# Fetching more table rows by address, and categories by one-hot products, in a deep-interest recommender kernel

## The chip, the cores and the metric

The kernel runs on one core of a Trainium2 chip. The metric is device time in microseconds (us) of one execution, the median of several. A core has five engines that run their own instruction streams: TensorE (PE, matrix products; PEld is its weight load), VectorE (DVE), ScalarE (ACT), GpSimd (POOL) and SyncE (SP). SP, ACT and POOL also issue DMAs.

## The reference

There are B = 16,384 users, each with a history of L = 200 items, one candidate item and one category; all are ids into tables of embeddings of D = 64 floats.

```python
def dice(x, alpha, axis):                 # normalised over the users
    mean = jnp.mean(x, axis=axis, keepdims=True)
    var = jnp.var(x, axis=axis, keepdims=True)
    p = jax.nn.sigmoid((x - mean) * jax.lax.rsqrt(var + EPS))
    return x * (p + alpha * (1.0 - p))
u, it, c, h = u_emb[user], i_emb[item], c_emb[cate], i_emb[hist]
itb = jnp.broadcast_to(it[None], h.shape)
feat = jnp.concatenate([h, itb, h - itb, h * itb], axis=-1)
a = dice(feat @ au_W1 + au_b1, au_alpha, axis=1)
w = a @ au_W2 + au_b2
cur = jnp.sum(w * jax.lax.stop_gradient(h), axis=0)
z = jnp.concatenate([u, it, c, cur], axis=-1)
z = dice(z @ W1 + b1, alpha1, axis=0)
z = dice(z @ W2 + b2, alpha2, axis=0)
return z @ W3 + b3
```

What matters here: 200 x 16,384 rows of 256 bytes come from the item table at random places (ids up to 100,000), and 16,384 each from the item, category and user tables once. The statistics of each l need all users of that l.

## The kernel before, in words

The users are 128 tiles of 128 rows. A step k takes 16 of them (TD = 16) for one l; 8 steps (ND = 8) make an l, and K = 1600 steps the loop. LAG = 10 further steps drain it.

Step k issues (`step`, L421): the id list of the next l (`load_hist_ids`), `fetch(k)` (L344), the load of the candidate rows of step k + 1 (`load_items`, L391, 512 KB from HBM by SP), `turn(k-1)` (L381: DVE transposes the rows into hT, ACT copies them to PSUM), `hidden` and `measure` of step k - 3 (L373, L376), once in 8 steps `moments` (L399: mean and variance, then `scale_and_shift` L166 with Sqrt on ACT), `gate(k-10)` (L350: two activations on ACT), `product(k-1)` (L394: PE, with DVE's product hm between its halves), and `weights` and `weigh` of step k - 10 (L355, L368, all on DVE). The schedule is manual: each engine runs its instructions in the order in which the code gives them.

A step's rows come in two ways. `gather` (L125) is an indirect DMA that POOL issues, 128 rows of 256 bytes by a column of ids. For three of the 128 tiles of each l (`SIDES`), rows come one by one by address: the ids are loaded on one partition (`load`, L293), DVE multiplies them by the row's size (`scale`, L296), the engine loads addresses into registers (L301) and issues one DMA of 256 bytes per row (L312 on SP, L323 on ACT). SP does two tiles of each l (`BY_SP`) and ACT one (`BY_ACT`); ACT then copies the finished tile into the step's buffer (L387). SP's rows use the eight rotating semaphores that its DMAs have; ACT's rows count into semaphores of their own (`landed`). ACT issues its rows in a step between `gate` and `product`. So 15 gathers are left in a step that has a side tile, and 16 in the others.

Before the loop (L474) 128 gathers fetch the candidates' rows into two buffers in turn, which are transposed, stored to HBM as `items`, and multiplied by their part of the first layer (`itp`). After it, the head fetches 16 groups of 16 gathers, categories and users in turn (`head_fetch`, L505), into three buffers, while the last steps drain. `head_layer` (L520) multiplies: for a category group the products of category, candidate and `cur`, for a user group those of the user and then the activations and statistics. The rest of the head (from L552) is a chain of normalisations, two dice layers, and the output DMAs.

Of the kernel before, what the change touches and what calls it, by code (L numbers as in the profile page):

```python
# [26 lines left out]
SIDES = (1, 5, 6)  # L27
PERIOD = 1
BY_SP = ((0, 1), (0, 5))
BY_ACT = ((0, 6),)  # L30
# [5 lines left out]
def din_kernel(  # L36
# [34 lines left out]
    NS = len(SIDES)  # L71
    NC = NT - NS
# [17 lines left out]
    def column(c, n):  # L90
        if c in SIDES and n == TD - 1:
            return NC + SIDES.index(c)
        return c * TD + n - sum(s < c for s in SIDES)

    def columns(v):
        return v[: NC * P].rearrange("(p n) -> p n", n=NC)

# [8 lines left out]
    items = [dram.tile([P, CD], F32, name=f"items{c}") for c in range(ND)]  # L106
    cur = [make(f"cur{c}", P, CD) for c in range(ND)]
# [5 lines left out]
    ucT = itp[:4]  # L113
    idx = [make(f"idx{i}", P, NT, dt=I32) for i in range(IDX)]
    ids = [make(f"ids{i}", P, NT, dt=I32) for i in range(3)]
    side = [make(f"side{i}", P, D) for i in range(3)]
    aside = [make(f"aside{i}", P, D) for i in range(2)]
    addr = [make(f"addr{i}", 1, P, dt=I32) for i in range(3)]
    aaddr = [make(f"aaddr{i}", 1, P, dt=I32) for i in range(2)]
    landed = [tc.alloc_semaphore(f"landed{i}") for i in range(2)]  # L120
# [12 lines left out]
    def load_ids(t, v):  # L133
        nc.sync.dma_start(t[:, :NC], columns(v))
        for s in range(NS):
            nc.sync.dma_start(t[:, NC + s : NC + s + 1], col(v[(NC + s) * P : (NC + s + 1) * P]))

    def load_hist_ids(i, l, by_address):
        nc.sync.dma_start(
            idx[i][:, :NC], r_hist[ds(l, 1), : NC * P].rearrange("l (p n) -> p (l n)", n=NC)  # L140
        )
        for s, c in enumerate(SIDES):
            if c not in by_address:
                j = NC + s
                nc.sync.dma_start(
                    idx[i][:, j : j + 1], r_hist[ds(l, 1), j * P : (j + 1) * P].rearrange("l p -> p l")
                )
# [18 lines left out]
    def scale_and_shift(mean, var, rstd, shift):  # L166
        n = mean.shape[0]
        std = small.tile([P, 1], F32, tag="std", name="std")
        nc.scalar.activation(std[:n], var, AF.Sqrt, bias=eps[:n])
        nc.vector.reciprocal(rstd, std[:n])  # L170
        nc.vector.scalar_tensor_tensor(shift, mean, -1.0, rstd, ALU.mult, ALU.mult)

    eps = make("eps", P, 1)
# [11 lines left out]
    def attention_weights():  # L185
        nc.vector.memset(eps, EPS)
# [36 lines left out]
    same_b = make("same_b", P, P)  # L223
    lanes, lane = (rows[-2].rearrange("p n d -> p (n d)")[:, (5 + i) * P : (6 + i) * P].bitcast(I32) for i in range(2))

    def head_weights():
# [21 lines left out]
        nc.sync.dma_start(bias3, b3.partition_broadcast(P))  # L248
        for t, u in ((ala, al1a), (alb, al1b), (al2, al12)):
            nc.vector.tensor_scalar(u, t, -1.0, 1.0, ALU.mult, ALU.add)  # L250
# [8 lines left out]
    class Queue:  # L259


        def __init__(self, engine, tiles, group, lead, span, buffers, addresses):
            self.engine, self.tiles, self.group, self.lead, self.span = engine, tiles, group, lead, span
            self.buffers, self.addresses, self.n = buffers, addresses, len(buffers)
            self.per = P // group
            self.plan = None

        def line(self, m):
            p, t = divmod(m, len(self.tiles))
            return p * PERIOD + self.tiles[t][0]  # L270

# [4 lines left out]
        def when(self, q):  # L276
            m, i = divmod(q, self.per)
            return m * PERIOD * ND // len(self.tiles) + i * self.span // self.per - self.lead

        def events(self, k, count):  # L280
            if self.plan is None:
                self.plan = {}
                for m in range(count):
                    at = self.when(m * self.per)
                    self.plan.setdefault(at - 8, []).append((self.load, m))
                    self.plan.setdefault(at - 5, []).append((self.scale, m))
                for q in range(count * self.per):
                    self.plan.setdefault(self.when(q), []).append((self.fetch, q))
            return self.plan.get(k, ())

        def load(self, m):
            j = NC + SIDES.index(self.tiles[m % len(self.tiles)][1])
            nc.sync.dma_start(self.addresses[m % self.n], r_hist[ds(self.line(m), 1), j * P : (j + 1) * P])  # L293

        def scale(self, m):
            nc.vector.tensor_scalar_mul(self.addresses[m % self.n], self.addresses[m % self.n], ROW)  # L296

        def fetch(self, q):
            m, part = divmod(q, self.per)
            p0 = part * self.group  # L300
            _, at = nc.values_load_multi_w_load_instructions(  # L301
                self.addresses[m % self.n][:, p0 : p0 + self.group],
                engines=(self.engine,), min_val=0, max_val=ROW * (V - 1),
                skip_runtime_bounds_check_because="the DMA checks the address against the table",
            )
            for j, a in enumerate(at):
                row = flat[ds(a, ROW)].rearrange("(o d) -> o d", o=1)
                self.start(m, self.buffers[m % self.n].bitcast(U8)[p0 + j : p0 + j + 1], row)

    class SyncQueue(Queue):  # L310
        def start(self, m, dst, row):
            nc.sync.dma_start(dst, row)  # L312

        def take(self, m):
            return self.buffers[m % self.n]

    class ScalarQueue(Queue):
# [3 lines left out]
        def start(self, m, dst, row):  # L321
            key = self.opened.setdefault(m, f"rows{next(self.names)}")
            dma = nc.scalar.dma_start(dst, row).then_inc(landed[m % self.n], 16)  # L323
            tc.no_tile_sem_insts.add(dma.ins.name)
            tc.add_to_no_dep_group(key, dma.ins)

        def take(self, m):
            fence = nc.scalar.wait_ge(landed[m % self.n], 16 * P)
            tc.declare_fence(fence.ins, group=self.opened.pop(m))
            nc.scalar.sem_clear(landed[m % self.n])  # L330
            return self.buffers[m % self.n]

    by_sync = SyncQueue(mybir.EngineType.SP, BY_SP, 16, 8, 4, side, addr)
    by_scalar = ScalarQueue(mybir.EngineType.Activation, BY_ACT, 8, 4, 8, aside, aaddr)
    queues = (by_sync, by_scalar)

    def by_address(l):
        return {c for q in queues for t, c in q.tiles if t == l % PERIOD}

    def has_side(k):  # L340
        l, c = divmod(k, ND)
        return c in by_address(l)

    def fetch(k):  # L344
        l, c = divmod(k, ND)
        for n in range(TD - has_side(k)):
            j = column(c, n)
            gather(rows[k % ROWS], idx[l % IDX][:, j : j + 1], n, i_emb)

    def gate(k):  # L350
        i = k // ND % 3
        nc.scalar.activation(pg, xs[k % XR], AF.Sigmoid, bias=shifts[i], scale=rstds[i])  # L352
        nc.scalar.activation(pg, pg, AF.Identity, bias=au_al, scale=au_1al)  # L353
# [27 lines left out]
    def turn(k):  # L381
        if has_side(k):
            l, c = divmod(k, ND)
            for q in queues:
                m = q.tile(l, c)
                if m is not None:
                    nc.scalar.copy(rows[k % ROWS][:, TD - 1], q.take(m))  # L387
# [11 lines left out]
    def moments(l):  # L399
# [17 lines left out]
        scale_and_shift(mean, var, rstds[i], shifts[i])  # L417
# [3 lines left out]
    def step(k):  # L421
# [4 lines left out]
        rows_by_scalar = ask(k)  # L426
        if has(k):
            l, c = divmod(k, ND)
            if c == 0 and l + 1 < L:
                load_hist_ids((l + 1) % IDX, l + 1, by_address(l + 1))  # L430
            fetch(k)
        if has(k + 1):
            load_items(k + 1)
        if has(k - 1):
            turn(k - 1)
        if has(k - 3):
            hidden(k - 3)
            measure(k - 3)
            if (k - 3) % ND == ND - 1:
                moments((k - 3) // ND)  # L440
        if has(k - LAG):
            gate(k - LAG)
        for q in rows_by_scalar:
            by_scalar.fetch(q)
# [6 lines left out]
    def ask(k):  # L451
        late = []
        for q in queues:
            for what, m in q.events(k, L * len(q.tiles) // PERIOD):
                if q is by_scalar and what == q.fetch:
                    late.append(m)
                else:
                    what(m)
        return late

    with tc.manual_schedule():
        load_ids(ids[0], r_item)
        load_hist_ids(0, 0, by_address(0))
        load_ids(ids[1], r_cate)
        load_ids(ids[2], r_user)
        nc.gpsimd.iota(lanes, pattern=[[1, P]], base=P, channel_multiplier=-1)
# [207 lines left out]
```

## Time and profile before

| | |
|---|---|
| Time, median of 3 runs | 31,799.49 us (31,797.17 to 31,803.53) |
| The profiled execution, its own time | 31,801.04 us |
| Its span, first to last instruction | 31,799.3 us |
| Busy: POOL, DVE, PE, ACT | 23,955.0, 22,816.1, 9,881.5, 6,126.3 us |
| POOL's gathers in the loop | 25,000 |
| POOL's gathers of candidates, categories, users | 128 each |
| Row DMAs by SP and by ACT | 51,200 and 25,600 |
| Item loads of 512 KB by SP | 1,608 |
| Granted TensorE clock, mean | 0.630 |

The profile shows one execution. A group's line gives the line of the code, the engine, the operation, what it writes and reads, how many, the busy time and mean of one, and the idle time of the engine just before them with what ended it ("issue": nothing that the profile shows was waited for). In the timeline a line has start, duration, engine, line and operation; neighbours of one kind are put together with their count, and SPq and ACTq are the issuing of DMAs. The waits view gives total us, times and the longest.

### The profile page before, as it was taken

How to read it: one execution, taken by the hardware profiler on the slowest of the kernel's cores; microseconds unless marked ns; L12 is line 12 of the kernel's file. 1: busy time of each engine (PE TensorE's matmuls, PEld its weight loads, DVE VectorE, ACT ScalarE, POOL GpSimd, SP SyncE). 2: the span in 40 equal slices, each digit the busy share in tenths (PEclk: the TensorE clock that was granted, in tenths of full speed). 3: DMA queues.
4: the chain of work that ended last, by engine and by line, in shares of the span. 5: the costliest groups of instructions: out<-in, count | busy, mean ns of one | idle time of the engine just before them, and what ended most of it. 6: DMA issues, size and time to landing. Idle time of an engine off the chain costs nothing.

```text
span 31799.3 us, 270304 instructions
## 1 busy us (share of the span) xinstructions
PE 9881.5 (31%) x13196; PEld 3707.9 (12%) x13196; DVE 22816.1 (72%) x32088; ACT 6126.3 (19%) x6061; POOL 23955.0 (75%) x25389
## 2 busy tenths in 40 slices
PE   2333333333333333333333333333333333333334
PEld 0111111111111111111111111111111111111111
DVE  5777777777777777777777777777777777777776
ACT  1111111111111111111111111111111111111111
POOL 7777777777777777777777777777777777777776
PEclk6666666666666666666666666666666666666666
DMA  2222222222222222222222222222222222222221
GB/s 56 55 54 55 55 54 55 55 55 55 54 55 55 55 54 55 55 55 54 55 55 55 54 55 55 54 55 55 55 54 55 55 55 54 55 55 55 54 55 41
DMA packets 1237919, 1731.75 MB, mean 54 GB/s; under 512 B 622320, under 2 KB 622920, under 8 KB 1235912
## 3 DMA queue, kind: packets, MB, share of 16 engines
q0 software_dynamic: 812288, 833.41, 15.1%
q1 hardware_dynamic: 371704, 874.34, 8.1%
q14 instruction: 1904, 15.60, 0.2%
q10 hardware_dynamic: 51920, 6.72, 0.1%
q8 instruction: 103, 1.69, 0.0%
HBM read 1708.09 MB, written 4.33 MB: 54 GB/s over the span
## 4 chain that ended last, share of the span: by engine, by line
POOL 59%; issue 22%; DMA 9%; DVE 7%; ACT 2%; SPq 1%; PE 0%; ACTq 0%; DVEq 0%; POOLq 0%
POOL rows L126 59%; DMA rows<-in_L_rec_i_emb,idx 9%; DVE hT L155 2%; DVE xs L374 1%; DVE st L379 1%; DVE pg L357 1%; ACT L352 1%; DVE py L358 1%; DVE py L356 1%; DVE py L370 1%; ACT pg L352 1%; ACT pg L353 1%; DVE pg L362 0%; DVE other L406 0%; SPq L312 0%
## 5 line engine op out<-in xcount | busy, mean ns | idle before, releaser
L126 POOL DMA_INDIRECT rows<-in_L_rec_i_emb,idx x25000 | 23592.1, 944 | 7625.2 <-issue 7297.1
L160 PE MATMUL px<-hT,blk_h 128*128 128x512 f32 x6400 | 5959.6, 1086 | 21047.3 <-DVE xs L374 21026.7
L155 DVE STREAM_TRANSPOSE hT<-rows 64x512 f32<-64x512 f32 x6400 | 4515.5, 706 | 7173.2 <-DMA rows<-in_L_rec_i_emb,idx 6913.2
L389 ACT COPY py<-hT 128x1024 f32<-128x1024 f32 x1600 | 1626.3, 1016 | 20747.7 <-DVE hT L155 20695.1
L160 PEld LDWEIGHTS px<-hT,blk_h 128*128 128x128 f32 x6400 | 1876.3, 323 | 24165.5 <-DVE xs L374 22491.3
L160 PE MATMUL px<-hm,blk_m 128*128 128x512 f32 x6400 | 3969.7, 753 | 519.7 <-DVE hm L396 519.7
L356 DVE TENSOR_TENSOR py<-pg,xs 128x1024 f32<-128x1024 f32 x1600 | 1972.6, 1233 | 594.6 <-ACT pg L353 446.9
L160 PEld LDWEIGHTS px<-hm,blk_m 128*128 128x128 f32 x6400 | 1757.4, 278 | 3422.8 <-issue 1871.7
L379 DVE BATCH_NORM_STATS2 st<-xs 128x6 f32<-128x512 f32 x3200 | 2058.5, 685 | 55.0
L357 DVE STREAM_TRANSPOSE pg<-py 128x1024 f32<-128x1024 f32 x1600 | 2024.5, 1265 | 55.5
L396 DVE TENSOR_TENSOR hm<-py,itT 128x1024 f32<-128x1024 f32 x1600 | 1932.7, 1208 | 147.8 <-DMA itT<-items 111.1
L358 DVE TENSOR_REDUCE py<-pg 128x32 f32<-128x1024 f32 x1600 | 1972.7, 1233 | 54.4
L370 DVE TENSOR_TENSOR py<-rows,pg 128x1024 f32<-128x1024 f32 x1600 | 1966.1, 1229 | 54.8
L371 DVE TENSOR_TENSOR cur<-py,cur 128x1024 f32<-128x1024 f32 x1600 | 1958.5, 1224 | 55.2
L374 DVE TENSOR_TENSOR xs<-px,itp 128x1024 f32<-128x1024 f32 x1600 | 1959.6, 1225 | 50.5
L352 ACT ACTIVATE pg<-xs,sh,rs 128x1024 f32<-128x1024 f32 x1600 | 1925.6, 1203 | 60.7 <-DVE py L370 58.1
L353 ACT ACTIVATE pg<-pg,au_al,au_1al 128x1024 f32<-128x1024 f32 x1600 | 1883.4, 1177 | 53.7
L362 DVE SCALAR_TENSOR_TENSOR pg<-py,au_bias,part 32x16 f32<-32x16 f32 x6400 | 1529.4, 239 | 225.6
L387 ACT COPY rows<-side 128x64 f32<-128x64 f32 x400 | 97.7, 244 | 2573.1 <-DMA side<-in_L_rec_i_emb 2559.8
L359 DVE COPY part<-py 64x32 f32<-64x32 f32 x1600 | 310.6, 194 | 55.5
L387 ACT COPY rows<-aside 128x64 f32<-128x64 f32 x200 | 48.8, 244 | 1265.4 <-DMA aside<-in_L_rec_i_emb 1265.4
L352 ACT ACT_TABLE_LOAD x200 | 256.6, 1283 | 3.5
(129 smaller groups left out, 1892.8 us busy)
## 6 DMA issues: line engine op xcount, KB each, us to landing
itT<-items SPq DMA_DIRECT2D x1608, 512.0 KB
side<-in_L_rec_i_emb SPq DMA_DIRECT2D x51200, 0.2 KB
aside<-in_L_rec_i_emb ACTq DMA_DIRECT2D x25600, 0.2 KB
rows<-in_L_rec_i_emb,idx POOLq DMA_INDIRECT x25000
idx<-in_r_hist SPq DMA_DIRECT2D x200, 62.5 KB
addr<-in_r_hist SPq DMA_DIRECT2D x400, 0.5 KB
items<-itT SPq DMA_DIRECT2D x8, 512.0 KB
aaddr<-in_r_hist SPq DMA_DIRECT2D x200, 0.5 KB
```

Source lines behind the costliest of these rows:

```text
L126: nc.gpsimd.indirect_dma_start(out=dst[:, n, :], out_offset=None, in_=table, in_offset=bass.IndirectOffsetOnAxis(ap=ids, axis=0),)
L155: nc.vector.transpose(by_tile(dst[ts(e, D)], i)[:, n0:n1], of[ts(i, D), n0:n1, ts(e, S)])
L160: nc.tensor.matmul(dst[:, ts(i, CH)], lhsT, rhs[:, ts(i, CH)], start=(first and j == 0), stop=(last and j == len(pairs) - 1), skip_group_c ...
L352: nc.scalar.activation(pg, xs[k % XR], AF.Sigmoid, bias=shifts[i], scale=rstds[i])
L353: nc.scalar.activation(pg, pg, AF.Identity, bias=au_al, scale=au_1al)
L356: nc.vector.tensor_mul(py, pg, xs[k % XR])
L357: nc.vector.transpose(pg, py)
L358: nc.vector.reduce_sum(total, pg.rearrange("p (n a) -> p n a", a=S), axis=mybir.AxisListType.X)
L370: nc.vector.tensor_mul(of, rows[k % ROWS], w.unsqueeze(2).to_broadcast([P, TD, D]))
L371: nc.vector.tensor_add(cur[k % ND], py, cur[k % ND])
L374: nc.vector.tensor_add(xs[k % XR], px[k % 2], itp[k % ND])
L379: nc.vector.bn_stats(stats[l % 3][:, 2 * c + i, :], xs[k % XR][:, ts(i, CH)])
```

## The change

**Rows by address.** The pattern repeats over four l (`PERIOD`): SP takes 11 tiles in it and ACT 11, so 5.5 tiles of each l. A step has at most one side tile. Addresses come in groups of 32 registers, rows are issued 7 steps ahead (`AHEAD`) at an even rate of 44 rows a step on each queue (`until`, `pump`), into 5 buffers per queue (`SLOTS`), with 4 id lists (`LISTS`). Id lists are now strided loads, since the tiles keep one common layout (which also takes the special columns out of `load_ids` and out of the output DMAs). On ACT, `gate` moves ahead of the turn, with 5 rows between its activations and 5 behind; the remaining rows follow the turn's copy. The copy of a finished tile is `place(k)`, in step k itself. In the step with `moments` the gate comes after them and after 20 rows.

**The root.** `root` computes 1/sqrt by an integer start and four Newton rounds, 15 small operations on DVE, in place of ACT's Sqrt and DVE's reciprocal.

**The categories.** They are no longer gathered in the head. In the prologue, between the candidates' groups, 16 halves (`category`) are each 2 products that spread the category numbers over the partitions, 16 comparisons on DVE that make ones and zeros, and 16 products of those with the table. The results are stored in HBM (`cates`) and loaded again in the head as `cT`. The candidates' rows take eight buffers rather than two.

**The head.** Eight groups of user gathers over four buffers; the products of what is known (`head_known`) and of the users (`head_users`) follow one another for each group; w1b's products come ahead of w1a's, and the first dice layer of group c + 1 is issued ahead of the products of group c.

```diff
-SIDES = (1, 5, 6)
-PERIOD = 1
-BY_SP = ((0, 1), (0, 5))
-BY_ACT = ((0, 6),)
+PERIOD = 4
+BY_SP = tuple((t, c) for t in range(PERIOD) for c in (0, 3, 6) if (t, c) != (3, 0))
+BY_ACT = tuple((t, c) for t in range(PERIOD) for c in (1, 4, 7) if (t, c) != (1, 1))
+GROUP = 32
+AHEAD = 7
+SLOTS = 5
+LISTS = 4
...
+    def root(dst, var):
+        n, w = var.shape
...
+        nc.vector.tensor_single_scalar(v, var, EPS, ALU.add)
+        nc.vector.tensor_single_scalar(t.bitcast(I32), v.bitcast(I32), 1, ALU.logical_shift_right)
+        nc.vector.tensor_scalar(dst.bitcast(I32), t.bitcast(I32), -1.0, float(0x5F3759DF), ALU.mult, ALU.add)
+        for _ in range(4):
+            nc.vector.tensor_mul(t, dst, dst)
+            nc.vector.scalar_tensor_tensor(t, t, -0.5, v, ALU.mult, ALU.mult)
+            nc.vector.scalar_tensor_tensor(dst, t, 1.5, dst, ALU.add, ALU.mult)
...
+        def until(self, k):
+            return min(self.total * P, max(0, int((k + AHEAD) * self.rate)))
+        def pump(self, upto):
+            while self.done < upto:
+                m, r = divmod(self.done, P)
+                if r % GROUP == 0:
+                    _, self.at = nc.values_load_multi_w_load_instructions(
+                        self.lists[m % LISTS][:, r : r + GROUP],
...
+                row = flat[ds(self.at[r % GROUP], ROW)].rearrange("(o d) -> o d", o=1)
+                self.start(m, self.slots[m % SLOTS].bitcast(U8)[r : r + 1], row)
+                self.done += 1
...
+    def place(k):
+        if side(k):
+            q, m = side(k)
+            nc.scalar.copy(rows[k % ROWS][:, TD - 1], q.take(m))
+    def gate(k, between):
...
+        between()
...
+        by_sync.pump(by_sync.until(k + 1))
+        norm = has(k - 3) and (k - 3) % ND == ND - 1
+        if has(k - LAG) and not norm:
+            gate(k - LAG, lambda: some(5))
+            some(5)
+        if has(k):
+            place(k)
         if has(k - 1):
             turn(k - 1)
         if has(k - 3):
             hidden(k - 3)
             measure(k - 3)
...
+        if norm:
+            moments((k - 3) // ND)
+            some(20)
+            if has(k - LAG):
+                gate(k - LAG, lambda: some(5))
+        by_scalar.pump(by_scalar.until(k + 1))
...
+    def category(c, i):
+        to = py[:, ts(i, CH)]
+        r = i * ND + c
+        for g in range(2):
+            said = pg[:, ts(g, CH)]
+            nc.tensor.matmul(
+                said.rearrange("p (n t) -> p n t", t=S), chosen[r // ND][:, r % ND],
+                numbers.rearrange("r (g t n) -> r g n t", g=2, n=TD)[:, g],
+                start=True, stop=True,
+            )
+            for k in range(NK):
+                ones = equal[next(turns_of_equal) % len(equal)]
+                nc.vector.tensor_scalar(ones, said, of_row[:, k : k + 1], None, ALU.is_equal)
+                nc.tensor.matmul(
+                    to, spread[k // 4][:, k % 4, g], ones,
+                    start=(g == 0 and k == 0), stop=(g == 1 and k == NK - 1),
+                )
+        nc.scalar.copy(xs[c % XR][:, ts(i, CH)], to)
...
-                    gather(rows[c % 2], ids[0][:, j : j + 1], n, i_emb)
+                    gather(rows[c], ids[0][:, j : j + 1], n, i_emb)
...
+            if c < ND:
+                category(*halves_of.pop(0))
+            before(c - ND - 1)
...
+        for c in range(ND):
+            nc.sync.dma_start(cates[c], xs[c % XR])
...
+        k, c = K, 0
+        for j in range(ND):
+            head_fetch(j)
+            nc.sync.dma_start(cT[j % 4], cates[j])
+            load_items(K + j)
+            while k <= K + (j + 1) * LAG // ND:
+                step(k)
+                k += 1
+            while c <= j and k > K + LAG - ND + c:
+                head_known(c)
+                head_users(c)
+                c += 1
```

More of the change, by code (lines that the diff above doesn't have):

```diff
@@ L112, in din_kernel @@
     itp = [make(f"itp{c}", P, CD) for c in range(ND)]
-    ucT = itp[:4]
+    uT, cT = itp[4:8], itp[:4]
     idx = [make(f"idx{i}", P, NT, dt=I32) for i in range(IDX)]
[L115 to L120, printed above, removed]
+    ids = [make(f"ids{i}", P, NT, dt=I32) for i in range(2)]
+    landed = [tc.alloc_semaphore(f"landed{i}") for i in range(SLOTS)]
     stats = [make(f"st{i}", P, 2 * ND, STATS) for i in range(3)]
@@ L424, in has, with some @@
             return 0 <= j < K
-        rows_by_scalar = ask(k)
+        def some(n):
+            by_scalar.pump(min(by_scalar.done + n, by_scalar.until(k + 1)))
+        for q in queues:
+            q.lead(k)
         if has(k):
@@ L449, in step @@
             weigh(k - LAG)
[L451 to L459, printed above, removed]
+    NK = -(-c_emb.shape[0] // P)
+    flat_tile = lambda t: t.rearrange("p n d -> p (n d)")
+    numbers = flat_tile(rows[8])[: 2 * ND]
+    chosen = [flat_tile(rows[9 + i])[: 2 * ND].rearrange("r (j m) -> r j m", m=P) for i in range(2)]
@@ L467, in din_kernel @@
         attention_weights()
[L468 to L469 removed]
+        category_numbers()
         for t in cur:
@@ L472, in din_kernel @@
         head_weights()
+        ahead = [-16]
+        halves_of = [(c, i) for c in range(ND) for i in range(2)]
         for c in range(ND + 1):
```

298 lines of the change are left out of this document (129 added, 169 removed).

## The prediction

> **What bounds the kernel now.** I read the page first: engine totals, the chain that ended last, the costliest group.
>
> ```profile
> span 31799.3 us, 270304 instructions
> PE 9881.5 (31%) x13196; PEld 3707.9 (12%) x13196; DVE 22816.1 (72%) x32088; ACT 6126.3 (19%) x6061; POOL 23955.0 (75%) x25389
> POOL 59%; issue 22%; DMA 9%; DVE 7%; ACT 2%; SPq 1%; PE 0%; ACTq 0%; DVEq 0%; POOLq 0%
> L126 POOL DMA_INDIRECT rows<-in_L_rec_i_emb,idx x25000 | 23592.1, 944 | 7625.2 <-issue 7297.1
> ```
>
> POOL is busy 75%, but the idle time ahead of its gathers is nearly all "issue": it waits for nobody. A gather therefore costs (23592.1 + 7625.2)/25000 = 1.2487 us, and 25,000 of them make 31,217.3 of the 31,799.3 us. Next the groups with shapes kept apart, for the gathers outside the loop:
>
> ```profile
> L126 POOL DMA_INDIRECT rows<-in_L_rec_i_emb,ids x128 | 120.9, 945 | 49.6 <-issue 36.9 <-DVE itT L155 9.3 <-DMA ids<-in_r_item 1.9
> L126 POOL DMA_INDIRECT rows<-in_L_rec_u_emb,ids x128 | 120.8, 944 | 39.0 <-issue 36.9 <-DMA rows<-in_L_rec_u_emb,ids 2.1
> L126 POOL DMA_INDIRECT rows<-in_L_rec_c_emb,ids x128 | 120.8, 944 | 39.0 <-issue 37.2 <-DMA rows<-in_L_rec_c_emb,ids 1.8
> ```
>
> These are 170.5, 159.8 and 159.8 us. With the loop: 31,707.4. One step of the loop in the timeline, then the waits, say what stands beside POOL:
>
> ```profile
> 10007.19 2.87 DVE L155 STREAM_TRANSPOSE hT<-rows 64x512 f32<-64x512 f32 x4 [5.56 <-DMA rows<-in_L_rec_i_emb,idx]
> ...
> 10012.28 1.18 ACT L353 ACTIVATE pg<-pg,au_al,au_1al 128x1024 f32<-128x1024 f32 x1
> ...
> 10013.14 6.32 ACTq L323 DMA_DIRECT2D aside<-in_L_rec_i_emb  x16
> ...
> 10014.95 2.85 PE L160 MATMUL px<-hm,blk_m 128*128 128x512 f32 x4
> ...
> 10020.29 1.22 DVE L371 TENSOR_TENSOR cur<-py,cur 128x1024 f32<-128x1024 f32 x1
> ...
> 10027.33 2.86 DVE L155 STREAM_TRANSPOSE hT<-rows 64x512 f32<-64x512 f32 x4 [5.82 <-DMA rows<-in_L_rec_i_emb,idx]
> ```
> ```profile
> SPq L392 <- DVE hm L396: 7403.9, 1381, 21.5
> DVE hT L155 <- DMA rows<-in_L_rec_i_emb,idx: 6913.2, 1459, 12.2
> SPq L312 <- DMA side<-in_L_rec_i_emb: 254.9, 781, 0.8
> ```
>
> DVE works from 10007.19 to 10021.51, 14.3 us, and then sits 5.82 us until the next gathers have landed: it has room. SP waits 7403.9 us, 4.63 us a step, for DVE before an item load: room too, and the question is whether the change uses it up.
>
> **The loop.** Before, 3 tiles of each l come row by row; now 5.5. That removes 2.5 x 200 = 500 gathers, 500 x 1.2487 = 624.3 us, if POOL stays the bound: 15.3125 gathers, 19.12 us a step, instead of 19.51. What pays is SP and ACT: 44 rows a step each, where they had 32 and 16. Their paces:
>
> ```profile
> 10013.69 2.11 ACTq L323 DMA_DIRECT2D aside<-in_L_rec_i_emb  x7
> 10015.49 5.34 SPq L312 DMA_DIRECT2D side<-in_L_rec_i_emb  x16
> 10133.21 12.35 SPq L312 DMA_DIRECT2D side<-in_L_rec_i_emb  x32
> ```
> ```profile
> L301 SPq TENSOR_LOAD <-addr x3200: 1132/1226/1472, 181.0 to 31191.3; - x189
> L301 ACTq TENSOR_LOAD <-aaddr x3200: 711/787/1017, 195.1 to 31301.8; - x189
> ```
> ```profile
> L392 SPq DMA_DIRECT2D itT<-items x1608: 319/360/394, 176.7 to 31585.2; - x179
> ```
> ```profile
> L136 SPq DMA_DIRECT2D ids<-in_r_item x3: 420/424/432, 1.2 to 2.2; - x3
> ```
>
> - SP: a row is 5.34/16 = 0.334 us while ACT issues as well. Addresses come in groups of 32 now: SP's 16 took 1.226 us and ACT's 8 took 0.787, so a register is about 0.055 us and a group of 32 about 2.1 us (estimate). 44 x 0.334 + 1.375 x (2.1 + 0.17 of gap, estimate) + 0.36 for the item load and as much as 0.17 around it + 0.344 lists at the 0.43 of L136's strided loads and the ids = 14.7 + 3.1 + 0.5 + 0.2 = 18.5 to 18.6 us. The bound is 19.12, so SP fits with 0.5 us to spare. The third row, 12.35 us for 32 with one register load of about 1.3 inside, gives 0.345 a row and 19.1 to 19.2 us: that end costs nothing to 130 us over the loop. I take 18.6, the pace of the commoner row. The 4.63 us wait for DVE that covered SP's work is then gone.
> - ACT: 2.11/7 = 0.30, with the gaps 0.3135 a row; 44 rows 13.8 us, registers 1.375 x 2.4 = 3.3, small things 0.4: 17.5. Its three large operations (3.4 us) are on top only if they do not run beside the issuing. The row above shows that they do: rows start at 10013.14, while L353 runs until 10013.46. The other end, all 3.4 us on top, is 20.9 us and would make ACT the bound; I take the first, since the row shows the overlap, and 5 rows are now put between and behind the activations.
> - DVE: `root` puts 15 small operations (about 3.0 us) where ACT's Sqrt was, and one list scaling per tile, about 0.5 us a step together, inside the 5.82 us of idle time. ACT loses two table loads per l, off the path: nothing.
> - Buffers: rows are asked for 7 steps ahead, with 5 buffers per queue; `place` takes them at step k. A late row would hold ACT, behind it the copy L389, and behind that the products and DVE; that is rival C.
>
> **The head.** The windows show 319 us of head gathers, then the end:
>
> ```profile
> 31389.00:31708.00 319.00, 148.85 (x256) 45.27 (x256) 163.47 (x238) 42.96 (x38) 241.08 (x256) 0.70 0.17 36
> 31708.00:31800.00 92.00, 56.28 (x116) 22.40 (x116) 55.45 (x81) 37.95 (x38) 0.54 (x1) 0.82 0.02 2
> ```
> ```profile
> 31403.57 1.22 DVE L371 TENSOR_TENSOR cur<-py,cur 128x1024 f32<-128x1024 f32 x1
> ...
> 31413.57 1.22 DVE L371 TENSOR_TENSOR cur<-py,cur 128x1024 f32<-128x1024 f32 x1
> ...
> 31426.71 1.23 DVE L356 TENSOR_TENSOR py<-pg,xs 128x1024 f32<-128x1024 f32 x1 [3.37 <-ACT pg L353]
> ...
> 31434.40 2.88 DVE L155 STREAM_TRANSPOSE hT<-cur 64x512 f32<-64x512 f32 x4
> ...
> 31442.75 1.02 PE L160 MATMUL px<-hT,w1b 128*32 128x512 f32 x2
> 31443.61 1.02 PE L160 MATMUL px<-itp,w1b 128*32 128x512 f32 x2
> ...
> 31718.02 1.28 DVE L503 BATCH_NORM_STATS2 zst<-rows 128x6 f32<-128x512 f32 x2 [0.97 <-ACT rows L531]
> ```
>
> 128 category gathers go, 159.8 us of POOL. But POOL then no longer sets the head's length. Its work without gathers, from the end G of the loop's gathers: step K 14.3, K+1 10.0 (the two L371 rows), K+2 some 20 (moments, `root`, an uncovered gate of 2.4, then 7.66 from 31426.71 to 31434.37), together 45. Then 8 tiles: a product (two instructions) takes 0.86 us by the starts of the two PE rows, a tile has 16, 13.7; with the transposes' first half (1.4), activation and statistics some 16.5. DVE meets the statistics before the next step's weights, so the 7 steps left, 8.3 each, add rather than overlap: 45 + 132 + 58 = 235. From the last statistics to the end it was 31799.3 - 31719.3 = 80.0; the earlier first `dice` gives some 5 back and `root` takes some 3: 78. So G + 313, where it was 319 + 92, 410 from G: a gain of 97, not 160.
>
> **The prologue.** 16 halves of 18 products at 0.86 with a copy are 17 us each (estimate), from about 33 us to about 320. POOL's step 8 wants a buffer that they use at 161 + 8 x 19.12 = 314. That is PE's pace in the head, where it is busy. In the loop, where it idles, the row at 10014.95 holds four instructions in 2.85 us with starts up to 0.86 apart: up to 1.7 a product, 31 us a half, an end near 530. I take the pace of the head, because PE would be busy here too, and a stall of 15 us; the ends are 0 and 215.
>
> **The sum.** Items 161.4 (the 9.3 wait goes with eight buffers) + 24,500 x 1.2487 = 30,593 + 1 of start: G = 30,755.5. Plus 313, plus 15: 31,083.5. The profiled execution was 31,801.04, 1.7 above its span: 31,085. The median was 31,799.49, 1.6 below that execution, which is less than I resolve.
>
> **The rivals.** Half a microsecond a step decides: from 19.12 us, each 0.1 us costs 160 us, and at 19.12 + (31,799 - 31,085)/1600 = 19.57 us all gain is gone.
>
> - **A, POOL still bounds**: 31,000 to 31,215. The bottom is the head with its 75 us of uncovered work hidden; the top adds 130 us, for SP at its slow row or six tenths of the way to the prologue's slow end.
> - **B, SP bounds mildly**, 19.2 to 19.5 us a step, or the prologue stalls by the full 200 us more (31,285): 31,215 to 31,735. For it: the 0.5 us of room is thinner than the spread of the rows. Against it: L312 waited only 254.9 us for its own landings.
> - **The change does not do what it says in the head**: the categories' saving is given back wholly, 31,182; inside A.
> - **C, slower: the rows of both queues share a way through the DMA that is narrower than their sum.** The best sustained pace of both together is the prologue's:
>
> ```profile
> 182.32 51.91 SPq L312 DMA_DIRECT2D side<-in_L_rec_i_emb  x128
> ...
> 249.26 38.43 SPq L312 DMA_DIRECT2D side<-in_L_rec_i_emb  x96
> ```
> ```profile
> 195.98 36.41 ACTq L323 DMA_DIRECT2D aside<-in_L_rec_i_emb  x80
> ```
> ```profile
> q1 hardware_dynamic: 371704, 874.34, 8.1%
> ```
>
> 128/51.91 + 80/36.41 = 4.66 rows a us. The 88 rows of a step need 4.60. If 4.66 were the ceiling and an item load shut it for 8.1% x 31,799/1608 = 1.6 us, a step would be 88/4.66 + 1.6 = 20.5 us, 1.36 over: 31,085 + 1600 x 1.36 = 33,260. It decides from 19.57 us. Against it: SP was no slower beside ACT (0.406 a row) than alone (0.400), so 4.66 is the pace of issue, and no row shows the ceiling itself. For it: 371,704 packets for 76,800 rows and 1,608 large loads are under five packets a row, so a row is not spread over 16 engines.
>
> [...]
>
> **How the numbers follow.** A 0.52, B 0.17, within 0.2% (63 us, what a measurement of this kernel can tell from no change) 0.04, C 0.27. So faster 0.69, same 0.04, slower 0.27. The likeliest is A: 31,085, its own range 31,000 to 31,215. C spreads from 31,863 to 33,260; cutting it at 32,200 leaves out 0.2, so the range is 31,000 to 32,200.
>
> **What would show it.** Right: about 24,500 loop gathers at 1.249 us each with "issue" ahead of them; DVE still waiting for gathers; SP's wait ahead of the item load shrunk to under 1 us a step; the head about 313 us long with DVE, PE and ACT in its chain. Wrong: idle time of POOL with a releaser other than issue, ACT waiting at `place` for rows, SP waiting for its own landings by more than 0.5 us a step (B or C), or a stall of POOL ahead of step 8 above 100 us.

## The result and the profile after

The changed kernel takes 33,151.59 us (median of 4 runs, 33,107.82 to 33,210.83), the kernel before 31,799.18 us (median of 4 runs): a ratio of 1.0426, with a 95% interval of 1.0405 to 1.0447. It is slower by 4.3%; 31,085 us was forecast, with a range up to 32,200.

The page of the changed kernel, in the order in which the one of before was read: span, engines, chain, and the costliest group.

```profile
span 33209.1 us, 401673 instructions
PE 10942.1 (33%) x13772; PEld 3750.7 (11%) x13772; DVE 23582.7 (71%) x35655; ACT 5713.1 (17%) x5969; POOL 23358.1 (70%) x24762
DMA 22%; DVE 20%; POOL 17%; SPq 16%; issue 13%; ACTq 8%; ACT 2%; PE 1%; DVEq 0%; POOLq 0%
L116 POOL DMA_INDIRECT rows<-in_L_rec_i_emb,idx x24500 | 23115.9, 944 | 9529.6 <-issue 7130.9
```

POOL does 500 gathers less, and a gather with its ordinary gap still costs 1.249 us. But POOL has fallen from 59% of the chain to 17%, and 9,529.6 us of idle time stand ahead of its gathers. Of these 7,130.9 are issue, its ordinary gap; 2,398.7 are put down to something else, where it was 328.1 before. Before, no gap was over 0.35 us; now the gaps exceed the ordinary 0.305 us by 2,051 us in all, 1,979 of them in the first line of the next view. What the others wait for, from the waits of all engines and then SP's own:

```profile
POOL rows L116 <- DVE py L367: 2128.8, 483, 15.2
DVE sp_lists L275 <- DMA sp_lists<-in_r_hist: 4434.9, 541, 12.7
DVE hm L387 <- DMA itT<-items: 1563.9, 295, 8.6
ACT rows L344 <- DMA sp_rows<-in_L_rec_i_emb: 791.0, 474, 16.2
```
```profile
SPq L301 <- DMA sp_rows<-in_L_rec_i_emb: 1294.7, 4654, 1.1
SPq L301 <- DMA itT<-items: 903.8, 1170, 1.8
SPq L383 <- DVE hm L387: 78.4, 8, 13.7
```

Read it backwards. POOL waits for buffers that DVE frees (L367). DVE waits for things that SP fetches: id lists (4,434.9 us) and item loads (1,563.9 us). And SP waits for nobody before its item load any more: the 7,403.9 us of before have become 78.4. What SP still waits for, in the middle of its work, are its own landings. SP's timeline shows it step by step (the 2.2 us ahead of the third group of rows are a load of registers, which the timeline leaves out):

```profile
15003.54 0.54 SPq L279 DMA_DIRECT2D sp_lists<-in_r_hist  x1
15004.17 0.55 SPq L279 DMA_DIRECT2D act_lists<-in_r_hist  x1
15004.82 0.54 SPq L383 DMA_DIRECT2D itT<-items  x1
15005.46 17.42 SPq L301 DMA_DIRECT2D sp_rows<-in_L_rec_i_emb  x44
15023.19 0.36 SPq L124 DMA_DIRECT2D idx<-in_r_hist  x1
15023.65 0.37 SPq L383 DMA_DIRECT2D itT<-items  x1
15024.13 17.93 SPq L301 DMA_DIRECT2D sp_rows<-in_L_rec_i_emb  x44
15042.23 0.36 SPq L383 DMA_DIRECT2D itT<-items  x1
15044.82 16.46 SPq L301 DMA_DIRECT2D sp_rows<-in_L_rec_i_emb  x44
...
15082.79 21.76 SPq L301 DMA_DIRECT2D sp_rows<-in_L_rec_i_emb  x44
```

One thing follows on the other, and 44 rows take from 16.46 to 21.76 us. From item load to item load it is 20.39 us in the mean of 1,520 steps, where POOL needs 19.12.

The time between the start of each of SP's instructions and the next, added up over those 1,520 steps in the trace, gives SP's step: rows 13.9 us, register loads 3.4, item load 0.65, lists 0.54, ids 0.1, and 1.7 us in which a row's DMA, all its addresses ready, waits for a semaphore; together 20.4. (The issue of the last row ahead of a load counts with that load.) Of the 1.7 us, 0.56 stand at the eighth row behind each item load (that row takes the semaphore of the load, which has not landed), the rest at all other rows.

The other two parts of the sum: POOL's first wait, at step 8 of the loop, in its timeline

```profile
314.04 0.94 POOL L116 DMA_INDIRECT rows<-in_L_rec_i_emb,idx  x1 [0.30 <-issue]
376.64 0.94 POOL L116 DMA_INDIRECT rows<-in_L_rec_i_emb,idx  x1 [61.66 <-PE pg L494]
```

is 61.7 us, with 7.3 more at step 19; 15 were forecast. The loop's last gather ends at 32,808.1, so the head is 33,209.1 - 32,808.1 = 401 us; 313 were forecast.

### The profile page after: what moved, and what is told of

Its sections match the earlier page's. It is cut to its first block, busy times and chain, and to the rows that moved or that the text cites. A ratio compares the mean times of both kernels' runs of the same rounds, so it can differ in the third digit from the quotient of the medians.

```text
span 33209.1 us, 401673 instructions
## 1 busy us (share of the span) xinstructions
PE 10942.1 (33%) x13772; PEld 3750.7 (11%) x13772; DVE 23582.7 (71%) x35655; ACT 5713.1 (17%) x5969; POOL 23358.1 (70%) x24762
## 3 DMA queue, kind: packets, MB, share of 16 engines
q0 software_dynamic: 792192, 812.79, 13.9%
## 4 chain that ended last, share of the span: by engine, by line
DMA 22%; DVE 20%; POOL 17%; SPq 16%; issue 13%; ACTq 8%; ACT 2%; PE 1%; DVEq 0%; POOLq 0%
POOL rows L116 17%; DMA sp_rows<-in_L_rec_i_emb 14%; SPq L301 10%; ACTq L301 7%; DVE hT L135 5%; SPq L291 5%; DMA itT<-items 4%; DMA rows<-in_L_rec_i_emb,idx 2%; DVE py L353 2%; DVE pg L354 2%; ACTq L291 2%; DMA act_lists<-in_r_hist 2%; DVE py L355 2%; DVE hm L387 1%; DVE xs L371 1%
## 5 line engine op out<-in xcount | busy, mean ns | idle before, releaser
L116 POOL DMA_INDIRECT rows<-in_L_rec_i_emb,idx x24500 | 23115.9, 944 | 9529.6 <-issue 7130.9
L140 PE MATMUL px<-hm,blk_m 128*128 128x512 f32 x6400 | 4610.8, 860 | 2748.1 <-DVE hm L387 2744.1
L387 DVE TENSOR_TENSOR hm<-py,itT 128x1024 f32<-128x1024 f32 x1600 | 1950.0, 1219 | 2902.9 <-DMA itT<-items 1563.9
L275 DVE TENSOR_SCALAR sp_lists<-sp_lists 1x128 int32<-1x128 int32 x551 | 139.8, 254 | 4435.0 <-DMA sp_lists<-in_r_hist 4434.9
L367 DVE TENSOR_TENSOR py<-rows,pg 128x1024 f32<-128x1024 f32 x1600 | 1966.3, 1229 | 54.9
L344 ACT COPY rows<-sp_rows 128x64 f32<-128x64 f32 x550 | 134.3, 244 | 946.6 <-DMA sp_rows<-in_L_rec_i_emb 791.0
L275 DVE TENSOR_SCALAR act_lists<-act_lists 1x128 int32<-1x128 int32 x551 | 135.3, 246 | 178.6 <-DMA act_lists<-in_r_hist 169.5
```

The lines of the kernel that those rows point to most:

```text
L116: nc.gpsimd.indirect_dma_start(out=dst[:, n, :], out_offset=None, in_=table, in_offset=bass.IndirectOffsetOnAxis(ap=ids, axis=0),)
L140: nc.tensor.matmul(dst[:, ts(i, CH)], lhsT, rhs[:, ts(i, CH)], start=(first and j == 0), stop=(last and j == len(pairs) - 1), skip_group_c ...
L367: nc.vector.tensor_mul(of, rows[k % ROWS], w.unsqueeze(2).to_broadcast([P, TD, D]))
L387: nc.vector.tensor_mul(hm[k % 2], py, itT[k % ITEMS])
```

## The experiments

Theory S: SP's instruction stream is the bound, because its rows wait for landings: in the traces of before and after its DMAs take eight semaphores in turn (103 to 110, and 106 to 113) and each waits for its own, so only eight can be under way. Theory D: the rows of both queues share something in the DMA that is full. Each of e1 to e4 is one execution beside the kernel before on the same chip, which took 31,828.21 us there.

### e1: the old share of rows

```diff
-PERIOD = 4
-BY_SP = tuple((t, c) for t in range(PERIOD) for c in (0, 3, 6) if (t, c) != (3, 0))
-BY_ACT = tuple((t, c) for t in range(PERIOD) for c in (1, 4, 7) if (t, c) != (1, 1))
+PERIOD = 1
+BY_SP = ((0, 1), (0, 5))
+BY_ACT = ((0, 6),)
```

> The changed kernel with the old share of rows by address: SP 2 tiles and ACT 1 of each l, all else as changed (categories in the prologue, root, new head). It has 25,000 loop gathers. Theory S (SP's issue stream sets the step of the changed kernel, because its rows wait for their own landings): with 16 or 32 rows a step POOL bounds again, the loop takes 25,000 x 1.2487 = 31,217 us, and head and prologue show what they are worth by themselves: 162 + 70 + 31,217 + 313 to 330 = 31,760 to 31,780 us. Theory D (the rows of both queues share a ceiling in the DMA): the same. If the head of 401 us is the head's own and not a consequence of the slow loop, it stays at 400 and the time is about 31,850.

Measured: 31,839.64 us. The page of e1:

```profile
span 31837.9 us, 268043 instructions
POOL 60%; issue 21%; DVE 8%; DMA 7%; PE 1%; ACT 1%; SPq 0%; DVEq 0%; POOLq 0%; ACTq 0%
L116 POOL DMA_INDIRECT rows<-in_L_rec_i_emb,idx x25000 | 23588.5, 944 | 7760.9 <-issue 7395.8
```

POOL bounds again. The loop's last gather ends at 31,511.9, so the head takes 326 us here: the 401 us of the changed kernel are 326 of the head's own and 75 brought along from the loop. The time is 60 to 80 us over what was expected, since POOL waits 134 us at the start and not 70, 129.5 of them at step 8; e1's prologue starts late (ACT's first copy of a half comes after 109.9 us of waiting), and why is open. The categories, the root and the new head, without the rows, came out 11 us slower than the kernel before beside them. Against the profile of before they take 410 - 326 = 84 us off the head and 9 off the candidates' part, and the loop with its wait takes 132 more.

### e2: semaphores of its own for SP's rows

```diff
-    landed = [tc.alloc_semaphore(f"landed{i}") for i in range(SLOTS)]
...
+            self.landed = [tc.alloc_semaphore(f"{name}_landed{i}") for i in range(SLOTS)]
+            self.opened = {}
...
-            dma = super().start(m, dst, row).then_inc(landed[m % SLOTS], 16)
+            dma = super().start(m, dst, row).then_inc(self.landed[m % SLOTS], 16)
...
-            fence = self.queue.wait_ge(landed[m % SLOTS], 16 * P)
+            fence = nc.scalar.wait_ge(self.landed[m % SLOTS], 16 * P)
...
-    by_sync = Queue("sp", mybir.EngineType.SP, nc.sync, BY_SP)
+    by_sync = Marked("sp", mybir.EngineType.SP, nc.sync, BY_SP)
```

> The changed kernel at the same 5.5 tiles of each l, but SP's rows count into five semaphores of their own, as ACT's do, instead of the eight rotating ones, so SP never waits for a landing before the next row. Theory S: the 1.7 us a step of waits go, SP needs 18.4 us a step, POOL bounds at 19.12, and the time is 162 + 70 + 30,593 + about 330 = 31,150 us (31,100 to 31,300). Theory D: rows land no faster; ACT waits at place instead, and the time stays within 33,000 to 33,300.

Measured: 31,955.08 us, 0.4% over before, and 19.57 us a step. Both expectations miss it. The chain of e2, waits of DVE and POOL, and SP's longest wait:

```profile
DMA 25%; POOL 21%; ACTq 20%; DVE 17%; issue 14%; ACT 2%; PE 1%; DVEq 0%; SPq 0%; POOLq 0%
```
```profile
DVE hT L134 <- DMA rows<-in_L_rec_i_emb,idx: 4415.1, 958, 10.6
POOL rows L115 <- DMA rows<-in_L_rec_i_emb,idx: 1388.6, 2597, 4.4
POOL rows L115 <- DVE py L367: 23.7, 34, 6.7
```
```profile
SPq L383 <- DVE hm L387: 1577.0, 310, 19.1
```

SP is out of the chain and has time left (it waits about 1 us a step for DVE again). So the eight semaphores did cost the changed kernel some 0.8 us a step, 1,200 us: theory S holds that far. But POOL now waits for its own gathers, 1,388.6 us where it was 273.6 before; less the ordinary gap of 0.305 us each time that is 597 us where it was none. The chain is led by gathers that are landing. For buffers that DVE frees, which a late ACT would hold too, POOL waits next to nothing beyond the ordinary gap (L367: 23.7 us, 2,128.8 in the changed kernel). That speaks against a rival reading of the 19.57 us, that ACT's own issue sets them. A gather counts its semaphore up 16 times, and the trace has the time of each count. Medians from issue, in us:

```
                      1st   8th   15th   16th   mean of the 16th
before               2.10  2.26   2.42   2.50   2.84
changed kernel       2.11  2.27   2.45   3.46   3.48
e2                   2.10  2.22   2.38   7.73   7.51
e3 (few item loads)  2.09  2.22   2.37   3.33   3.32
e4 (4.5 tiles)       2.10  2.22   2.36   3.00   3.05
```

The medians of the first, the eighth and the fifteenth count agree within 0.1 us in all kernels, and only the last is late. By the packets of its queue in the trace a gather is sixteen of 2,048 bytes and sixteen of 4 (406,144 of each for the 25,384 gathers of before), so there is a count for each sixteenth of the data. One count late and fifteen on time fit one DMA engine with a queue in front of it and fifteen with none; that is the author's reading, and no view names an engine. The last count is late the more, the more rows by address there are and the faster they come (3.00, 3.46 and 7.73 us in e4, the changed kernel and e2): that fits theory D, and by this reading one engine is the thing that is shared. With SP's brake taken off, a step of 88 rows, a load and 15.3 gathers takes 19.57 us, and POOL waits for landings in it.

### e3: item loads left out

```diff
-        if has(k + 1):
+        if has(k + 1) and k < 3:
             load_items(k + 1)
```

> The changed kernel with the item loads left out from step 4 on (the loop then multiplies by old candidate rows, so that part of the computation is wrong). Theory S: SP loses 0.45 us of issue, the 0.56 us a step for the semaphore that the load shares with a row, and a part of the other 1.15 us of landing waits: a step of 18.5 to 19.4 us, so 31,150 to 31,650 us. Theory D in its form with a load that shuts the way for 1.6 us: 88/4.66 = 18.9 a step, POOL bounds, 31,150.

Measured: 31,182.44 us, 2.0% below the kernel before. Page and SP's own waits:

```profile
span 31180.7 us, 396887 instructions
L116 POOL DMA_INDIRECT rows<-in_L_rec_i_emb,idx x24500 | 23145.9, 945 | 7546.6 <-issue 7182.4
```
```profile
SPq L301 <- DMA sp_rows<-in_L_rec_i_emb: 1017.4, 4134, 0.7
```

POOL bounds with 19.14 us a step and 24,500 gathers. ACT's rows, register loads and activations are those of the changed kernel and, but for one wait and one clearing of a semaphore for each of SP's tiles, of e2. So ACT by itself needs no more than 19.14 us for 44 rows. What e3 takes away is about 0.5 us a step of SP's issue, the 903.8 us at the load's semaphore, and, under theory D, the load's share of what is full. That suffices, under both theories, so e3 does not tell them apart; it shows that the 88 rows alone fit.

### e4: 4.5 tiles of each l

```diff
-BY_SP = tuple((t, c) for t in range(PERIOD) for c in (0, 3, 6) if (t, c) != (3, 0))
-BY_ACT = tuple((t, c) for t in range(PERIOD) for c in (1, 4, 7) if (t, c) != (1, 1))
+BY_SP = tuple((t, c) for t in range(PERIOD) for c in (0, 3, 6) if c != 0 or t == 0)
+BY_ACT = tuple((t, c) for t in range(PERIOD) for c in (1, 4, 7) if c != 1 or t == 2)
```

> The changed kernel with 9 tiles in four l by SP and 9 by ACT instead of 11 each, 4.5 of each l, 36 rows a step and queue (and each id list loaded once only). Theory S: SP needs 36 x 0.323 + 1.125 x 2.5 + 1.0 + about 1.5 of waits = 16.9 us a step; POOL bounds with 15.4375 gathers, 19.28 us a step, 162 + 70 + 30,843 + 330 = 31,405 us. Theory D: 72/4.66 + 1.6 = 17.1, the same. Either says faster than before; a time above 31,800 would speak against both.

Measured: 31,415.91 us, 11 us from the sum. (The edit also keeps an id list from being loaded twice, which the changed kernel does for 2 of its 552 lists on each queue.) It beats both kernels: 412 us or 1.3% below the kernel before on the same chip (one execution each).

```profile
span 31414.1 us, 348161 instructions
POOL 58%; issue 22%; DVE 10%; DMA 7%; PE 1%; ACTq 1%; ACT 1%; DVEq 0%; SPq 0%; POOLq 0%
L116 POOL DMA_INDIRECT rows<-in_L_rec_i_emb,idx x24700 | 23334.7, 945 | 7591.7 <-issue 7307.2
```
```profile
SPq L387 <- DVE hm L391: 4682.1, 1449, 24.9
SPq L305 <- DMA itT<-items: 942.3, 1167, 3.2
SPq L305 <- DMA sp_rows<-in_L_rec_i_emb: 509.9, 1947, 1.0
```

SP has 4,682.1 us left, 2.9 us a step; its waits for its own rows are 509.9 us instead of 1,294.7, for 18% fewer rows. The head is 325 us, the prologue's wait 54.6.

### e5 to e12: the room between 72 and 88 rows, and the late count

Five further kernels were run on other chips (three of them twice), where the kernel before took 48,341 us (e5 to e8) and 47,978 us (e9 to e12). On those chips SP and ACT issue in stretches at 0.7 us an instruction, and the kernel before takes half as long again as on the first ones. So their times say nothing of the two theories. They are told for what their counts of packets and e12's price of issue show. Where the expectations of e5 and e12 speak of a gather's engines, the traces show its counts.

```diff
 # e5, e9: e2 and e3 together
 # e6, e10: 5.0 tiles of each l
+BY_SP = tuple((t, c) for t in range(PERIOD) for c in (0, 3, 6) if c or t % 2 == 0)
+BY_ACT = tuple((t, c) for t in range(PERIOD) for c in (1, 4, 7) if c != 1 or t % 2)
 # e7, e11: this BY_SP with the BY_ACT of the changed kernel; e8: e6 with the semaphores of e2
 # e12: e2, and each row in two pieces
-            self.slots = [make(f"{name}_rows{i}", P, D) for i in range(SLOTS)]
+            self.slots = [make(f"{name}_rows{i}", P, 2, S + 8)[:, :, :S] for i in range(SLOTS)]
...
-                row = flat[ds(self.at[r % GROUP], ROW)].rearrange("(o d) -> o d", o=1)
+                row = flat[ds(self.at[r % GROUP], ROW)].rearrange("(o h d) -> o h d", o=1, h=2)
```

> e2 and e3 together: 5.5 tiles of each l, SP's rows on semaphores of their own, and no item loads from step 4 on (old candidate rows are used, so that part of the computation is wrong). With semaphores of its own SP was rid of its waits, yet a step took 19.57 us; a gather's first DMA engine landed after 2.10 us as ever, its last after 7.7 us instead of 2.5. Theory D, refined: one of the DMA engines carries all rows of both queues and its share of gathers and item loads, and is full at 19.57 us a step with 88 rows. Without the loads it has room: the landing falls back below 4 us, POOL bounds at 19.12, 31,150 to 31,250 us. Rival A: ACT's own issue, with activations and copies between its rows, needs 19.6 us a step; then nothing changes, 31,900 to 32,000.

> The changed kernel with 10 tiles in four l by SP and 10 by ACT, 5.0 of each l, 40 rows a step and queue, eight rotating semaphores as in the changed kernel. SP: 40 x 0.323 + 1.25 x 2.5 + 1.0 + 1.6 of landing waits = 18.6 us; POOL 15.375 x 1.2487 = 19.20. If the waits stay at 1.7 us, POOL bounds: 163 + 55 + 30,718 + 326 = 31,265 us (31,230 to 31,350). If the waits grow with the load as steeply as between e4 and the changed kernel, SP needs 19.3 to 19.6 us and the time is 31,400 to 31,900.

> SP 10 and ACT 11 tiles in four l, 5.25 of each l, 84 rows a step. POOL 15.3438 gathers, 19.16 us a step, 31,200 us if it bounds. SP as in e6 with a little more waiting, 18.7 to 19.2 us. [...] So 31,200 to 31,300 us, faster than before by 1.6 to 2.0%; over 31,500 would say that the room ends already below 84 rows.

> e6 with SP's rows on semaphores of their own. POOL bounds in any theory with the engine's share at 80 rows about 18.2 us: 31,265 us, as e6 if e6 has room; a gather's last landing at some 3 to 4 us in the mean.

Measured: e5 53,050.9, e6 53,066.49, e7 51,329.25 (ratio 1.0617, 1.0599 to 1.0635), e8 53,071.43 us.

> The kernel of e5 once more, since the chip of that job issued SP's and ACT's instructions in stretches at 0.7 us each and gave the kernel before 48,341 us. 5.5 tiles of each l, SP's rows on semaphores of their own, no item loads from step 4 on (old candidate rows are used). Theory D: one DMA engine is full at 19.57 us a step in e2; without the loads it has room, POOL bounds at 19.12, 31,150 to 31,250 us, and a gather's last count comes below 4 us. Rival A, ACT's own issue needs 19.6 us: 31,900 to 32,000.

> The kernel of e6 once more, for the same reason. 5.0 tiles of each l, eight rotating semaphores: POOL bounds, 31,230 to 31,350 us; if SP's waits for its own landings grow steeply between 72 and 88 rows a step, 31,400 to 31,900.

> The kernel of e7 once more, for the same reason. 5.25 tiles of each l, 84 rows a step: 31,200 to 31,300 us if POOL bounds; over 31,500 if the room ends below 84 rows.

> e2 with each row by address as two pieces of 128 bytes, with a gap between them at the destination, so that the transfer has an outer dimension of 2 on both sides. In e2 the first 15 of a gather's 16 counts come between 2.10 and 2.38 us (medians) and the 16th at 7.73: one engine lags. If the outer dimension decides how many engines carry a row, two engines carry it now and the 15th count lags as well. If an engine's time goes by pieces, each of the two has as many as the one had and the step stays at 19.4 to 19.7 us, 31,700 to 32,200; if it goes by bytes, the lag shrinks, POOL bounds and the time is 31,150 to 31,250. If nothing of this is so, only the 16th lags, with twice the pieces, and the step is far over 20 us.

Measured: e9 52,751.22, e10 52,928.63, e11 51,116.58 (ratio 1.0656, 1.0638 to 1.0673), e12 81,829.92 us. The rows of L305 in e6 show the disturbance: a median of 228 ns as ever, and a maximum of 1,488 for an instruction that took at most 761 in the changed kernel; even a register move, 29 ns, takes up to 1,500.

```profile
L305 SPq MOVE sp_rows<-in_L_rec_i_emb x64000: 1/29/1500, 251.1 to 52633.5; - x200
L305 SPq DMA_DIRECT2D sp_rows<-in_L_rec_i_emb x64000: 1/228/1488, 251.2 to 52633.6; - x200
```

Two things can be read from e12. One is its queues, which do not depend on the pace. ACT's queue in e2, where a row is one piece, and then in e12:

```profile
q10 hardware_dynamic: 141376, 18.37, 2.7%
```
```profile
q10 hardware_dynamic: 282176, 18.65, 0.2%
```

ACT issues 70,400 rows: two packets each in e2 (in the trace one of 256 bytes, the data, and one of 4, the count) and four in e12 (two of 128 and two of 4). A count does not go with every piece: an item load has 128 packets of 4,096 bytes and sixteen of 4 (before). So the shape of a row's transfer changes its number of counts, one in one piece and two in two halves. That a count stands for an engine, and that a row in one piece goes through one, is the author's reading, which the trace doesn't show. Which counts lag in e12 can't be read: 88 rows have about 51 us there (81,829.92 us over 1,600 steps, estimate), and its trace has only 32,701 of the gathers' 396,096 counts. In e2 the same queue's packets took 2.7% of the time of 16 engines, in the changed kernel 0.4%, which fits packets that had to queue.

The other is what a row in two pieces costs its issuer. A row's DMA on SP in e9, where it is one piece, and then in e12, on the same chip:

```profile
L302 SPq DMA_DIRECT2D sp_rows<-in_L_rec_i_emb x70400: 1/227/1512, 249.8 to 52384.3; - x200
```
```profile
L302 SPq DMA_DIRECT2D sp_rows<-in_L_rec_i_emb x70400: 1/625/2196, 250.0 to 81404.4; - x200
```

The median goes from 227 ns to 625. The slow stretches don't make it: 14% of SP's moves fall in them in both kernels, and of e12's row DMAs behind a move of ordinary length, nineteen in twenty take 0.56 us or more. At 0.56 us, 44 rows would be at least 24.7 us of issue a step (estimate). So rows in halves, whatever they do for the landings, are no way to 88 rows in 19.12 us. The price of issue also explains most of the 29,078 us between e12 and e9: 0.4 us more for each of SP's 70,400 rows is 28,000 (e9 leaves out the item loads besides).

## Why the prediction was wrong

- **The gather's price, right.** 1.249 to 1.250 us a gather, with issue ahead of it, wherever POOL did not wait (the changed kernel, e1, e3 and e4), whatever SP and ACT did. e3 has nearly the loop that was forecast, 30,593 us: at 1.250 us a gather 30,624, plus a wait of 68 in the prologue; its 31,182 us lie in the likeliest range, but it leaves the item loads out.
- **The step that failed: "44 x 0.334 + 1.375 x (2.1 + 0.17 of gap, estimate) + ... = 18.5 to 18.6 us. The bound is 19.12, so SP fits".** Measured 20.39. Rows and register loads were 17.8 in the sum and are 17.35; what is missing are the landing waits, 1.7 us, for which the sum has no term, and small things: lists 0.54 for 0.15, since SP loads ACT's lists too (0.69 a step and not 0.344) and one costs 0.79 with what stands around it, and the item load 0.65 for 0.5. The waits were seen and waved off, "L312 waited only 254.9 us for its own landings", 0.16 us a step. That was the wait at 48 rows a step, and the load's semaphore added 0.05. By the waits view the two are 0.32 and 0.59 us at 72 rows (e4), and 0.81 and 0.56 at 88; over 0.5 us was the prediction's own sign of being wrong, and it came. The rows land later: from a row's issue by SP to its count the trace has 1.98 us in the mean before, 2.37 in e4 and 2.62 in the changed kernel, and eight rows at 0.32 us each are 2.6. 1,600 x 1.24 us (20.36 instead of 19.12 over the whole loop) is 1,983 us, nearly all of the miss.
- **Rival C, the right side, and the right price by luck.** It gave 33,260; measured 33,151.59. Its ceiling, 4.66 rows a us, was only the pace of issue: 88 rows, 15.3 gathers and a load pass in 19.57 us (e2), and without loads 88 rows fit into POOL's 19.14 (e3). The mechanism, as far as the runs show it, is in two parts. With more rows a gather's last count comes later, at 3.46 us and not at 2.50, and at 7.73 in e2, which fits a shared way that is nearly full, as C says. And rows land later (2.62 us and not 1.98), so that SP, with eight DMAs under way, waits for them. The second part turns 19.57 into 20.39: SP as the bound, which was rival B's mechanism, at a price beyond its 19.5. The 1.36 us a step that C took from a ceiling of issue and a load that shuts the way are 1.24 from other things. C's count of packets was misread too: the 371,704 are SP's queue alone, with 51,200 rows and not 76,800; its conclusion holds, since a row has two packets. That the thing shared is one engine was not shown: one late count of sixteen fits it, and so do the two counts of a row in e12.
- **"Against it: SP was no slower beside ACT": a true row, a wrong use.** In those stretches of the prologue there are no item loads. The rows showed that the DMA kept up with 4.66 rows a us for 36 us, not that it does with loads and the loop's gathers between.
- **ACT, right.** Its activations run beside its rows (e3: POOL bounds with ACT at 44 rows).
- **The break-even of 19.57 us, right by chance.** e2 has that step to the hundredth, and came out 0.4% over before: its wait in the prologue is 73 us and not 15, its head 327 and not 313.
- **The head: 313 forecast, 325 to 327 in the four kernels where POOL or the DMA sets the step (e1 to e4).** The term is 12 to 14 us short. The 401 us of the changed kernel are not the head's: DVE was steps behind when POOL finished, and in POOL's timeline the user gathers wait 68 us for buffers. The gain of the head, 84 us, is most of the 97 expected, not the 160 of the gathers removed.
- **The prologue: 15 us forecast, 69 measured, 68 and 55 in e3 and e4.** The mis-sized term is a half's time: 17 us by PE's products; from 325.06 to 366.05 DVE's comparisons of two halves show 20.5 each, and all sixteen took from 26 to 391, 22.8 each. The 16 comparisons take 0.74 us each, and DVE and PE wait for one another at every change of group. It lies between the 17 that were taken and the 31 of the slow end.

What stays open: whether e2's 19.57 us falls to POOL's 19.12 without loads, as theory D says (e5, e9), where between 72 and 88 rows a step the room ends (5.0 and 5.25 tiles), and whether two counts lag when rows come in halves. Each was run, on chips that did not let it be read. No run says how the 19.57 us of e2 divide into rows, loads and gathers, and none shows the 18.2 us that e8's expectation takes for an engine's share at 80 rows: what is shown is 19.57 us a step with 88 rows and loads (e2) and POOL's 19.14 without loads (e3).

## What to carry to other kernels

A queue that fits by its issue times may still not fit by its landings: count how many of its DMAs can be under way, multiply by the pace that is wanted, and compare it with the time to land, at the load that the change will make and not at the one before. Eight semaphores at one row in 0.32 us bear 2.6 us of landing; SP's rows landed in 2.0 us in the mean before the change and in 2.6 after it, a quarter of them in more than 3.2. And look at each count of a transfer: fifteen of a gather's sixteen came by 2.45 us in the changed kernel and by 2.38 in e2 (medians), and the last at 3.46 and 7.73.

## What the runs showed of the hardware

- The 16 counts of one gather come within 0.4 us of each other in the kernel before (2.10 to 2.50), and in the changed kernel the last comes 1 us behind the others (2.45 us for the 15th, 3.46 for the 16th). One engine with a queue would fit it, but no view names an engine. The mean busy share of all 16 engines, 2 tenths in nearly every slice of the pages of before and after, does not show it.
- A row that shared a rotating semaphore with an item load of 512 KB waited for that load: in the changed kernel the eighth row behind each load waited 0.56 us in the mean, the seven ahead of it 0.01 to 0.03.
- A register load of 32 addresses took 2.12 us on SP (median, e4 and the changed kernel), as estimated from the smaller ones (2.1).
- A row of 256 bytes in two pieces of 128 took SP 0.625 us to issue (e12, median) and in one piece 0.227 (e9, the same chip).
- On two other chips the kernel before took 48,341 and 47,978 us instead of 31,800. There 16% of SP's and 14% of ACT's register moves took over 0.3 us (e6), at 0.7 us mostly and on both engines in the same stretches; in e4, on the chip of e1 to e4, none did. The cause is open. More rows on SP and ACT cost 6% (5.25 tiles) to 10% (5.0 tiles) over the kernel before there; why fewer rows cost more is open too.
